# A two-layer RWKV block with an FP4 feed-forward on one core: three branches' second products in one burst, sums by channel block, pair products two levels at a time

## The chip, the cores and the metric

The kernel runs on one core of a Trainium2 chip. The metric is the device time of one execution in microseconds (us), the median of several runs. Engines are named as in the profile: PE is TensorE (PEld its weight loads), DVE is VectorE, ACT is ScalarE, POOL is GpSimd, SP is SyncE, which issues the DMAs.

## The reference

The input x is 2 x 4096 x 256, all in float32. It is normalised and modulated (`adaLN`), passed through two RWKV layers (a time mix and a channel mix each), added back with a gate, normalised again, and passed through a gated feed-forward whose inputs and weights are quantised to FP4 in blocks of 16 and dequantised. Cut to what matters here, a time mix is:

```python
sx = shift(x) - x
mix = tanh((x + sx * x_maa) @ tm_w1)              # 5 branches of E = 32 columns
mw, mk, mv, mr, mg = mix_f @ tm_w2[f]             # 32 -> 256, once for each branch f
wx = x + sx * (w_maa + mw)                        # and kx, vx, rx, gx likewise
r, k, v, g = sigmoid(rx @ Wr), kx @ Wk, vx @ Wv, silu(gx @ Wg)
w = exp(-exp(time_decay + tanh(wx @ td_w1) @ td_w2))
# for each head of 64 channels, step by step over t:
out_t = r_t @ (state + u * k_t^T v_t);  state = state * w_t + k_t^T v_t
h = h + (groupnorm(out) * g) @ Wo
```

The products `mix_f @ tm_w2[f]` are the "second products" of the title. The recurrence over t is what the pair products replace.

## The kernel before

**Tiles.** The work is cut into blocks of 256 time steps (`TT`), 16 for each of the two batches; each block passes both layers, so there are 64 time mixes and 64 channel mixes, and 32 feed-forwards in 64 chunks. A working tile ("slot", 128 partitions x 514 float32) holds one block in channel-major or time-major form; there are 36 slots, 4 double ones (`stock2`), 5 longer ones (`long`) and some tiny ones. PSUM has five banks that are handed out (`bank`), two banks for the pair products (`pa`) and one for `kv`.

**The planner.** Nothing is issued where it is written. Streams (one for each batch and layer, one for the feed-forward's inputs, one for each of its two chunks, one for its weights) record operations through `pl.tensor`, `pl.vector` and so on; `Plan.run` then gives them out one at a time by an estimate of when each could start (`weight`, `LAT`, `SAME`, `TURN`). Consecutive recordings on `pl.tensor` make one operation, a burst, which is given out whole and needs all its banks at once. The order of each engine's queue is therefore fixed when the kernel is built. Eight plans with different random ranks (`PLANS`, `JITTER`) are tried, and the one with the lowest estimated end is used. Because every operation is issued by `record` and `give_out`, the profile shows one line number (L294) for all of them, and the tiles' names tell them apart.

**Second products** (`time_mix`, L1006 to L1031). After the tanh, `mix_s` holds branches w, k, v, r in four groups of 32 partitions (`mixa`) and four copies of branch g (`mixb`). Three bursts follow: g's two products (one for each half of the output channels, in row groups 0 and 1, in two banks), `branch_pair(0, 3, ...)` for w and r (four products in row groups 0 and 3, two banks), and later `branch_pair(1, 2, ...)` for k and v. Each branch then goes through `to_input`: two SCALAR_TENSOR_TENSORs on DVE that read the bank, and one 128x512 sum on POOL that adds x.

**Pair products** (`wkv`, L837 to L965). A block of 128 steps is split into halves level by level (seven levels, h = 1, 2, ... 64). At each level PE multiplies r and k of paired halves into `pa`, and then DVE multiplies the r of each second half and the k of each first half by accumulated decays in place (`upd`). The products of a level have to read r and k before that level's update changes them, and after the update of the level before. The lines that set the bursts are these:

```python
        for l in range(7):
            h = 1 << l
            for m in {0: (), 1: (0, 1)}.get(l, (l,)):
                products(m)
```

Levels 0 and 1 share a burst, because level 0 reads copies of r and k with the bonus (`r0`, `k0`, two slots); levels 2 to 6 have one burst each. Levels 1 to 4 have 64 matmul records to a burst, level 5 has 32, level 6 has 16. Masks are applied by DVE (COPY_PREDICATED into `diag`) after levels 3 and 6. Only one block at a time is in this part (`head_lock`); its r and k lie in a double slot from `Wr`'s projection to the end of `wkv`.

**Channel mix and feed-forward** (L1125 to L1160, L1306 to L1394) are projections on PE with activations and FP4 steps (`fp4`, five DVE passes and one on ACT). `fp4` uses one `long` tile as scratch, and a chunk's hidden values and their transposes lie in two more.

## Time and profile before

| | |
|---|---|
| median of 3 runs | 3125.28 us (3124.25 to 3128.61) |
| the profiled execution | 3123.61 us |
| its span, first to last instruction | 3121.7 us |
| granted TensorE clock, mean | 0.981 |
| PE busy (matmul records) | 2984.9 us, 96%, 38460 records |
| PEld busy | 2412.9 us, 77% |
| DVE busy | 2365.4 us, 76%, 6146 instructions |
| ACT busy | 1615.4 us, 52%, 3362 instructions |
| POOL busy | 940.6 us, 30%, 888 instructions |

Busy times are unions over one profiled execution, from the first to the last instruction; 1.9 us of that execution lie outside the span. A float32 product shows as two matmul records. Matmuls are pipelined and their ends are modelled, so the time that a run of them takes is read from the start of its first to the start of whatever follows it. The span's first 60 us are mostly loads and the conditioning; the last 60 us are the last feed-forward chunks.

### The profile page before, as it was taken

Reading aid. Unit: us, or ns where it says so; the run is one execution under the profiler, and the core shown is the slowest. Engines: PE = TensorE matmul, PEld = TensorE weight load, DVE = VectorE, ACT = ScalarE, POOL = GpSimd, SP = SyncE. Lnnn points to the kernel's source line nnn. Section 1 sums busy time; section 2 is a strip of 40 time slices with the busy share of each in tenths; the row PEclk is TensorE's granted clock in tenths of the full one; section 3 lists DMA queues with packets and bytes.
Section 4 is the critical chain, followed back from the end, with each engine's and each line's share of the span. In section 5 each row is a group of like instructions: output and inputs, shape, how many; then the busy total and the mean of one; then the engine's idle time right before and its main releaser. Section 6 shows DMA issues by size and latency. Waiting matters only on the chain. (4 is left out here: it accounts for less than half of the span.)

```text
span 3121.7 us, 89338 instructions
## 1 busy us (share of the span) xinstructions
PE 2984.9 (96%) x38460; PEld 2412.9 (77%) x38460; DVE 2365.4 (76%) x6146; ACT 1615.4 (52%) x3362; POOL 940.6 (30%) x888
## 2 busy tenths in 40 slices
PE   6899999999999999999999999999999999999997
PEld 4777778778787777877778787787878778787775
DVE  6785778777877777778777787777777778766877
ACT  3565555545555556455454655546445455455442
POOL 2233323223233332332323233232332323331220
PEclk9899999999999999999999999999999999999989
DMA  4000000000000000000000000000000000000000
GB/s 141 20 14 5 10 7 15 7 15 7 9 12 7 16 8 11 11 6 17 5 11 11 5 18 5 14 8 9 13 6 17 5 8 15 9 9 9 8 13 11
DMA packets 35725, 42.53 MB, mean 14 GB/s; under 512 B 2817, under 2 KB 33537, under 8 KB 35329
## 3 DMA queue, kind: packets, MB, share of 16 engines
q1 hardware_dynamic: 35328, 36.81, 3.7%
q8 instruction: 302, 4.95, 0.7%
q14 instruction: 95, 0.77, 0.1%
HBM read 28.41 MB, written 8.39 MB: 12 GB/s over the span
## 5 line engine op out<-in xcount | busy, mean ns | idle before, releaser
L294 POOL TENSOR_TENSOR slot<-slot,slot 128x512 f32<-128x512 f32 (+1 forms) x448 | 508.9, 1152 | 961.5 <-DVE slot L294 682.0
L294 ACT ACTIVATE slot<-bank 128x512 f32<-128x512 f32 (+2 forms) x644 | 331.6, 519 | 682.8 <-PE bank L294 661.1
L294 POOL TENSOR_TENSOR tiny<-tiny,nhalf 128x2 f32<-128x2 f32 (+1 forms) x288 | 289.3, 1009 | 869.6 <-DVE tiny L294 789.4
L294 DVE TENSOR_TENSOR slot<-slot,slot 128x512 f32<-128x512 f32 x512 | 372.1, 728 | 110.2 <-PE pa L294 79.6
L294 PE MATMUL bank<-slot,small 32*128 32x256 f32 (+3 forms) x2816 | 393.3, 361 | 8.9 <-DVE slot L294 4.4
L294 PE MATMUL bank<-slot,cWk 128*128 128x256 f32 x1536 | 367.9, 385 | 2.5 <-DVE slot L294 2.0
L294 PE MATMUL bank<-cWv,slot 128*128 128x256 f32 x1536 | 343.8, 380 | 0.0
L294 PEld LDWEIGHTS pa<-slot 64*32 64x32 f32 x19456 | 224.0, 109 | 154.2 <-DVE diag L294 54.2
L294 PEld LDWEIGHTS bank<-slot,small 32*128 32x128 f32 (+3 forms) x2816 | 272.3, 178 | 88.3 <-issue 33.8
L294 PEld LDWEIGHTS bank<-slot,cWk 128*128 128x128 f32 x1536 | 284.5, 191 | 46.9 <-DVE slot L294 4.3
L294 PEld LDWEIGHTS bank<-cWv,slot 128*128 128x128 f32 x1536 | 289.2, 190 | 39.8 <-issue 0.3
L294 PE MATMUL pa<-slot 64*32 64x16 f32 x19456 | 266.2, 191 | 43.0 <-DVE diag L294 23.7
L294 ACT ACTIVATE slot<-bank,small 128x256 f32<-128x256 f32 (+1 forms) x640 | 248.4, 449 | 111.6 <-PE bank L294 109.9
L294 DVE SCALAR_TENSOR_TENSOR slot<-bank,small,slot 128x256 f32<-128x256 f32 x640 | 271.8, 473 | 24.9 <-PE bank L294 23.9
L294 DVE TENSOR_TENSOR slot<-slot,bank 128x512 f32<-128x512 f32 x192 | 131.0, 682 | 189.3 <-PE bank L294 143.0
L294 POOL TENSOR_TENSOR slot<-slot 128x512 f32<-128x512 f32 x128 | 141.9, 1111 | 346.8 <-ACT slot L294 272.3
L294 ACT ACTIVATE slot<-slot 128x512 f32<-128x512 f32 x288 | 181.3, 633 | 42.8 <-DVE slot L294 38.0
L294 DVE TENSOR_TENSOR long<-long,bank 128x352 f32<-128x352 f32 x256 | 131.1, 514 | 93.0 <-ACT long L294 69.8
L294 DVE SCALAR_TENSOR_TENSOR slot<-slot,small,slot 128x256 f32<-128x256 f32 x384 | 186.7, 518 | 16.8 <-POOL slot L294 16.7
L294 PE MATMUL bank<-ident,slot 128*128 128x128 f32 x1152 | 178.0, 283 | 14.0 <-ACT slot L294 8.6
L294 ACT COPY slot<-bank 128x512 f32<-128x512 f32 x224 | 130.3, 586 | 111.3 <-PE bank L294 107.3
L294 PE MATMUL bank<-wd,long 128*128 128x256 f32 x768 | 184.7, 391 | 1.2 <-ACT long L294 1.2
(106 smaller groups left out, 5362.5 us busy)
## 6 DMA issues: line engine op xcount, KB each, us to landing
slot<-in_L_attn_x_dram SPq DMA_DIRECT2D x64, 256.0 KB, 2.7
out_dram<-slot SPq DMA_DIRECT2D x64, 128.0 KB, 1.7
slot<-in_L_wmod_dram SPq DMA_DIRECT2D x6, 256.0 KB, 7.7
cWk<-in_L_attn_cWk_dram SPq DMA_DIRECT2D x2, 768.0 KB, 8.2
cWv<-in_L_attn_cWv_dram SPq DMA_DIRECT2D x2, 768.0 KB, 9.4
small<-in_small_dram SPq DMA_DIRECT2D x2, 718.0 KB, 8.3
long<-in_L_ffn_w_down_dram SPq DMA_DIRECT2D x2, 352.0 KB, 2.8
long<-in_L_ffn_w_gate_dram SPq DMA_DIRECT2D x5, 128.0 KB, 7.2
```

What stands on the lines that cost most here:

```text
L294: fn(*[real(v) for v in a], **{n: real(v) for n, v in k.items()})
```

## The change

- The second products of g, w and r are recorded as one burst of six products in row groups 1, 0 and 3 and in three banks, one bank for each branch; g now uses row group 1 for both halves of the channels. k and v stay a burst of their own. `to_input`'s sum on POOL is made for each half of the channels (two instructions of 128x256 in place of one of 128x512).
- In `wkv`, the products of levels 2 and 3 are one burst, and those of levels 4 and 5 another. For that the r and k from before an update must outlive it: the updates of level 2 and of level 4 write into another tile (`rk2`, kept for all blocks, in which level 0's copies lie too), and ACT copies the halves that the update does not touch. The other updates stay in place.
- Slots are reused in place where a result could overwrite an input (`x_s = xn_s`, `g_s = xg_s`, `hT_s = hb_s` and others), the counts of tiles go from 36, 4 and 5 to 37, 3 and 4, and streams that find no double or long tile wait.
- The planner's estimates of latencies change, and one plan is made in place of eight.

The diff, cut:

```diff
-SLOTS = 36
+SLOTS = 37
-PLANS, JITTER = 8, 8.0
-SLOTS2 = 4
+PLANS, JITTER = 1, 8.0
+SLOTS2 = 3
-LONG = 5
+LONG = 4
...
-    LAT = {"tensor": 170.0, "vector": 0.0, "scalar": 0.0, "gpsimd": 0.0, "sync": 2600.0, "load": 0.0}
+    LAT = {"tensor": 170.0, "vector": 120.0, "scalar": 60.0, "gpsimd": 200.0, "sync": 2600.0, "load": 0.0}
...
-    SAME = {"vector": 34.0, "scalar": 25.0, "gpsimd": 80.0}
+    SAME = {"vector": 84.0, "scalar": 25.0, "gpsimd": 80.0}
...
+        w["w2"] = [w2a[E * f : E * (f + 1), :] for f in range(4)] + [w2b[E : 2 * E, :]]
...
+    rk2 = keep.tile([P, 2 * J * TT], F32, name="rk2")
...
+    def pair_view(rk, h, n, changed=True):
+        v = rk[:, h : h + 1] if changed else rk[:, :1]
+        return bass.AP(
+            v.tensor, v.offset, [v.ap[0], [J * TT - h if changed else J * TT + h, 2], [2 * h, n], [1, h]]
+        )
...
-        r0_s, k0_s = take_slot(), take_slot()
-        r0, k0 = v4(r0_s), v4(k0_s)
+        r0, k0 = parts(rk2)
+        r, k = parts(rk)
...
+        place = {0: rk2, 1: rk, 2: rk, 3: rk2, 4: rk2, 5: rk, 6: rk, 7: rk}
         def products(l):
-            R, K = (r0, k0) if l == 0 else (r, k)
+            R, K = parts(place[l])
...
-            for m in {0: (), 1: (0, 1)}.get(l, (l,)):
+            for m in {1: (0, 1), 3: (2, 3), 5: (4, 5), 6: (6,)}.get(l, ()):
                 products(m)
...
-            upd = pair_view(rk, h, n)
+            here, there = place[l] if l else rk, place[l + 1]
+            if here is not there:
+                pl.scalar.copy(pair_view(there, h, n, False), pair_view(here, h, n, False))
             pl.vector.tensor_tensor(
-                upd, upd, tv...to_broadcast([P, 2, n, h]), ALU.mult
+                pair_view(there, h, n), pair_view(here, h, n), tv...to_broadcast([P, 2, n, h]), ALU.mult
             )
...
-            pl.gpsimd.tensor_tensor(m, m, x, ALU.add)
+            for j in range(J):
+                pl.gpsimd.tensor_tensor(m[:, j, :], m[:, j, :], x[:, j, :], ALU.add)
...
+        def branches(es, places):
+            bks, os = zip(*(pl.bank() for _ in es))
             for j in range(J):
-                for e, o in zip((f, g), os):
+                for e, o in zip(es, os):
+                    rows_, mix = (slice(E * e, E * (e + 1)), mixa) if e < 4 else (slice(E, 2 * E), mixb)
                     mm(
-                        o[:, j * TT : (j + 1) * TT], w["w2"][e][:, j * P : (j + 1) * P],
-                        mixa[E * e : E * (e + 1), :], True, True,
+                        o[:, j * TT : (j + 1) * TT], w["w2"][e][:, j * P : (j + 1) * P], mix[rows_, :],
+                        True, True,
                     )
...
-        bks, os = zip(*(pl.bank() for _ in range(2)))
-        for j in range(J):
-            js = slice(j * E, (j + 1) * E)
-            mm(os[j][:, :TT], w["w2b"][js, j * P : (j + 1) * P], mixb[js, :], True, True)
-        xg_s = to_input([o[:, :TT] for o in os], w["g_maa"])
...
-        xw_s, xr_s = branch_pair(0, 3, w["w_maa"], w["r_maa"])
+        xg_s, xw_s, xr_s = branches((4, 0, 3), (None, None, None))
+        yield
...
-        xk_s, xv_s = branch_pair(1, 2, w["k_maa"], w["v_maa"])
-        give(mix_s, x_s, sx_s)
+        xk_s, xv_s = branches((1, 2), (None, sx_s))
+        give(mix_s, x_s)
+        while not stock2:
+            yield
...
-        hT_s = pl.take(long)
+        hT_s = hb_s
```

More of the change, by code (lines that the diff above doesn't have):

```diff
@@ L600, in rwkv_adaln_fp4_kernel @@
         at += J * ED
-        w2a, w["w2b"], w["td2"] = (small[:, at + m * D : at + (m + 1) * D] for m in range(3))
-        w["w2"] = [w2a[E * f : E * (f + 1), :] for f in range(4)]
+        w2a, w2b, w["td2"] = (small[:, at + m * D : at + (m + 1) * D] for m in range(3))
+        w["w2"] = [w2a[E * f : E * (f + 1), :] for f in range(4)] + [w2b[E : 2 * E, :]]
         for n in ("Wr", "Wk", "Wv", "Wg", "Wo"):
@@ L763, in shifted @@
         bk, pt = to_channels(xn)
-        x_s = take_slot()
+        x_s = xn_s
         xT = x_s.rearrange("p (j t) -> p j t", j=J)
@@ L769, in shifted @@
         pl.close(bk)
-        give(xn_s)
         pl.vector.tensor_copy(car, xT[:, :, TT : TT + 1])
@@ L776, in shifted, with lerp @@
         return xT[:, :, 1:], sx, x_s, sx_s
-    def lerp(x, sx, maa):
-        m_s = take_slot()
+    def lerp(x, sx, maa, m_s=None):
+        m_s = m_s or take_slot()
         m = v3(m_s)
@@ L803, in proj_tok, with parts @@
         return bk, o
-    def pair_view(rk, h, n):
-        v = rk[:, h : h + 1]
-        return bass.AP(v.tensor, v.offset, [v.ap[0], [J * TT - h, 2], [2 * h, n], [1, h]])
+    def parts(rk):
+        return (
+            rk[:, m * J * TT : (m + 1) * J * TT].rearrange("p (c j t) -> p c j t", c=C, j=J) for m in range(2)
+        )
[3 more added lines that the diff above has]
+            v.tensor, v.offset, [v.ap[0], [J * TT - h if changed else J * TT + h, 2], [2 * h, n], [1, h]]
+        )
     def with_bonus(dst, src, odd, u):
@@ L840, in wkv @@
         rk = rk_s[:, : 2 * J * TT]
-        r, k = (rk[:, m * J * TT : (m + 1) * J * TT].rearrange(
-            "p (c j t) -> p c j t", c=C, j=J) for m in range(2))
         dec, v = v4(dec_s), v3(v_s)
@@ L878, in wkv @@
             h = 1 << l
-            for m in {0: (), 1: (0, 1)}.get(l, (l,)):
+            for m in {1: (0, 1), 3: (2, 3), 5: (4, 5), 6: (6,)}.get(l, ()):
                 products(m)
-            if l == 1:
-                give(r0_s, k0_s)
             n = C * J * P // (2 * h)
             tv = tot.rearrange("p (n two) -> p n two", two=2)
-            upd = pair_view(rk, h, n)
+            here, there = place[l] if l else rk, place[l + 1]
+            if here is not there:
+                pl.scalar.copy(pair_view(there, h, n, False), pair_view(here, h, n, False))
             pl.vector.tensor_tensor(
-                upd, upd, tv.rearrange("p n m -> p m n").unsqueeze(3).to_broadcast([P, 2, n, h]), ALU.mult
+                pair_view(there, h, n), pair_view(here, h, n), tv.rearrange("p n m -> p m n").unsqueeze(3).to_broadcast([P, 2, n, h]), ALU.mult
             )
@@ L915, in wkv @@
         give(dec_s)
+        r, k = parts(rk)
         tot = tot.rearrange("p (c j) -> p c j", c=C)
@@ L987, in time_mix @@
             mm(pm[:, TT : 2 * TT], w["w1"][:, k, P:], xx[:, k, :], k == 0, k == J - 1)
-        give(xx_s)
-        mix_s = take_slot()
+        mix_s = xx_s
         mixa, mixb = mix_s[:, :TT], mix_s[:, TT : 2 * TT]
@@ L993, in time_mix, with to_input @@
         yield
-        def to_input(o, maa):
-            m_s = take_slot()
+        def to_input(o, maa, m_s=None):
+            m_s = m_s or take_slot()
             m = v3(m_s)
@@ L1002, in to_input @@
                 )
-            pl.gpsimd.tensor_tensor(m, m, x, ALU.add)
-            return m_s
-        def branch_pair(f, g, maa_f, maa_g):
-            bks, os = zip(*(pl.bank() for _ in range(2)))
+            for j in range(J):
+                pl.gpsimd.tensor_tensor(m[:, j, :], m[:, j, :], x[:, j, :], ALU.add)
+            return m_s
+        def branches(es, places):
+            bks, os = zip(*(pl.bank() for _ in es))
             for j in range(J):
-                for e, o in zip((f, g), os):
-                    mm(
-                        o[:, j * TT : (j + 1) * TT], w["w2"][e][:, j * P : (j + 1) * P],
-                        mixa[E * e : E * (e + 1), :], True, True,
+                for e, o in zip(es, os):
+                    rows_, mix = (slice(E * e, E * (e + 1)), mixa) if e < 4 else (slice(E, 2 * E), mixb)
+                    mm(
+                        o[:, j * TT : (j + 1) * TT], w["w2"][e][:, j * P : (j + 1) * P], mix[rows_, :],
+                        True, True,
                     )
             ms = []
-            for bk, o, maa in zip(bks, os, (maa_f, maa_g)):
-                ms.append(to_input([o[:, j * TT : (j + 1) * TT] for j in range(J)], maa))
+            for e, bk, o, s in zip(es, bks, os, places):
+                ms.append(to_input([o[:, j * TT : (j + 1) * TT] for j in range(J)], w["wkvrg"[e] + "_maa"], s))
                 pl.close(bk)
             return ms
-        bks, os = zip(*(pl.bank() for _ in range(2)))
-        for j in range(J):
-            js = slice(j * E, (j + 1) * E)
-            mm(os[j][:, :TT], w["w2b"][js, j * P : (j + 1) * P], mixb[js, :], True, True)
-        xg_s = to_input([o[:, :TT] for o in os], w["g_maa"])
-        for bk in bks:
-            pl.close(bk)
+        xg_s, xw_s, xr_s = branches((4, 0, 3), (None, None, None))
         yield
-        xw_s, xr_s = branch_pair(0, 3, w["w_maa"], w["r_maa"])
         bk, pg = proj(w["Wg"], v3(xg_s))
-        give(xg_s)
-        g_s = take_slot()
+        g_s = xg_s
         g_t = v3(g_s)
@@ L1046, in time_mix @@
                 )
-        give(xw_s)
-        td_s = take_slot()
+        td_s = xw_s
         td = td_s[:, :P]
@@ L1096, in time_mix @@
             )
-        v_s = take_slot()
+        v_s = xv_s
         xv = v3(xv_s)
@@ L1101, in time_mix @@
         pl.close(bk)
-        give(xv_s)
         yield
@@ L1106, in time_mix @@
         bk, pt = to_channels(v3(o_s))
-        give(o_s)
-        oT_s = take_slot()
+        oT_s = o_s
         oT = v3(oT_s)
@@ L1128, in channel_mix @@
         xk, xk_s = lerp(x, sx, w["ck_maa"])
-        xr, xr_s = lerp(x, sx, w["cr_maa"])
-        give(x_s, sx_s)
+        xr, xr_s = lerp(x, sx, w["cr_maa"], sx_s)
+        give(x_s)
         yield
@@ L1139, in channel_mix @@
                     mm(o[:, m, :], w["cWk"][:, k, n0 : n0 + P], xk[:, k, :], k == 0, k == J - 1)
-            kks.append(take_slot())
+            kks.append(take_slot() if g < FD // P // 2 - 1 else xk_s)
             kg = v3(kks[-1])
@@ L1145, in channel_mix @@
             yield
-        give(xk_s)
-        sr_s = take_slot()
+        sr_s = xr_s
         sr = v3(sr_s)
@@ L1151, in channel_mix @@
         pl.close(bk)
-        give(xr_s)
         yield
@@ L1317, in ffn_inputs @@
             yield from layernorm_rows(x1, xn, rows["cb"][b], lambda c: rows["sb"][b])
+            while not long:
+                yield
             p_s = pl.take(long)
@@ L1320, in ffn_inputs @@
             long.append(p_s)
-            xq_s = take_slot()
+            xq_s = xn_s
             xqT = v3(xq_s)
@@ L1325, in ffn_inputs @@
             pl.close(bk)
-            give(xn_s)
             left = []
@@ L1345, in ffn_chunk @@
         x1, xqT = v3(x1_s), v3(xq_s)
+        while not long:
+            yield
         hb_s = pl.take(long)
@@ L1362, in ffn_chunk @@
             yield
+        while not long:
+            yield
         p_s = pl.take(long)
@@ L1377, in ffn_chunk @@
             yield
-        long.append(hb_s)
         bk, y = pl.bank()
```

## The prediction

> **What bounds the kernel now.** I read the page first, then the busy time by stage, then PE's timeline at places where the changed bursts stand alone, then the groups by shape. From the page:

> ```profile
> span 3121.7 us, 89338 instructions
> PE 2984.9 (96%) x38460; PEld 2412.9 (77%) x38460; DVE 2365.4 (76%) x6146; ACT 1615.4 (52%) x3362; POOL 940.6 (30%) x888
> PE   6899999999999999999999999999999999999997
> PEclk9899999999999999999999999999999999999989
> ```

> PE is at 9 in all but the first two slices and the last, and its clock is granted. The busy time by stage says how much of the rest can still be filled:

> ```profile
> 0.00:60.00 60.00, 33.87 (x298) 20.36 (x299) 34.31 (x111) 15.15 (x33) 12.95 (x34) 0.89 0.50 176
> 60.00:200.00 140.00, 124.00 (x1792) 100.91 (x1781) 112.53 (x326) 74.76 (x165) 45.15 (x41) 0.94 0.07 19
> 200.00:2900.00 2700.00, 2634.78 (x34827) 2138.58 (x34808) 2050.71 (x5330) 1438.80 (x2995) 838.81 (x772) 0.99 0.03 10
> 2900.00:3060.00 160.00, 148.32 (x1425) 120.32 (x1424) 125.88 (x298) 73.86 (x145) 37.63 (x36) 0.93 0.03 10
> 3060.00:3122.00 62.00, 43.98 (x176) 32.77 (x174) 41.96 (x83) 12.88 (x25) 6.05 (x8) 0.89 0.04 13
> ```

> The columns are length, then busy time of PE, PEld, DVE, ACT, POOL, then clock. Between 200 and 2900 us PE is without work for 65 us of 2700 (2.4%); the start costs 42 us and the last 222 us cost 30. So the time is PE's queue, and what counts is how long a burst keeps PE, start to start. PE's timeline (start, length, run) shows that:

> ```profile
> 424.13 0.70 PE L294 MATMUL bank<-slot,small 32*128 32x256 f32 x4
> 424.76 1.99 PE L294 MATMUL bank<-Wv,slot 128*128 128x256 f32 x8
> ...
> 427.12 1.13 PE L294 MATMUL bank<-slot,small 32*128 32x256 f32 x8
> 428.19 0.48 PE L294 MATMUL bank<-slot,Wg 128*128 128x256 f32 x1
> ```

> ```profile
> 546.71 1.89 PE L294 MATMUL bank<-slot,cWk 128*128 128x256 f32 x8
> 548.54 0.73 PE L294 MATMUL pa<-slot 64*32 64x16 f32 x64
> 549.20 1.45 PE L294 MATMUL bank<-wg,slot 128*128 128x352 f32 x4
> ```

> ```profile
> 1505.88 1.89 PE L294 MATMUL bank<-slot,small 128*128 128x256 f32 x8
> 1507.61 1.35 PE L294 MATMUL bank<-wg,slot 128*128 128x352 f32 x4
> ```

> g's burst alone (x4, two products side by side) takes 0.63 us; four products in two row groups (x8) take 1.06, that is one more round of 0.43. A level's pair products (x64) take 0.66. Eight full records take 1.73 ahead of full records and 1.83 ahead of a burst of another shape: entering a burst costs 0.10. The joint burst of levels 0 and 1 shows in the busy time of `pa` alone, 128 records from 586.82 to the next run at 588.03:

> ```profile
> 586.82:588.02 1.20, 1.20 (x128) 1.18 (x128) 0.00 (x0) 0.00 (x0) 1.00 0.05 14
> ```

> [...]

> **Second products.** Counted over the trace's records, the 64 time mixes make 18 runs of four records (g alone), 74 of eight, 40 of twelve and 7 longer, so g's burst stands alone 18 times and next to another one of its shape 46 times. In the new burst g's products run in a third row group beside w's and r's, and the burst should stay at 1.06. Saved: 18 x (0.63 + 0.10) + 46 x 0.43 = 33 us. That three groups run abreast is not shown by this shape. Bounds: if only two do, six products need three rounds, and what goes is the separate entry and tail, 18 x (0.73 - 0.43) = 5 us; if all do, 33. I take 33: the nearest row is `pa`'s, whose 64 records in 64x32 pieces (two row groups by four column groups) start every 8.6 ns (0.55 us for 64), far beyond two abreast.

> The burst needs three banks at once. That costs nothing as long as five are enough; the cover is that 46 of 64 times g's and the next burst already ran back to back with four banks between them, and PE's idle time before this shape is 3.7 us in all. Should the cover fail, every burst would wait for one bank's two DVE reads, 64 x 0.95 = 61 us, all of the gain.

> **Pair products.** A joint burst saves 0.66 + 0.66 - 1.21 = 0.11 us of tail, and one entry of 0.10. The trace holds 365 bursts on `pa` (some of the 384 already touch another); four for each of 64 blocks leave 256. 109 x 0.21 = 23 us. Waits go with the bursts: single-level ones lose 0.09 us each (0.08 ahead, 0.01 inside), joint ones of levels 0 and 1 also 0.09 (half ahead, half inside), so 109 x 0.09 = 10 us at most; since a joint burst waits for the later of two inputs I take 5. Bounds for both together: 7 (each new joint burst idles 0.12 inside, the mean of joint bursts over their median, 128 x 0.12 off 23) to 33; 28 taken.

> What these bursts wait for now is seen in the waits (total, times, longest):

> ```profile
> POOL slot L294 <- DVE slot L294: 691.8, 169, 22.9
> DVE slot L294 <- PE pa L294: 84.5, 92, 4.9
> PEld pa L294 <- DVE diag L294: 54.2, 81, 2.3
> ```

> DVE waits for the products before it may overwrite r and k (second line). With the second tile the updates of levels 2 and 4 wait for no burst, so two of six round trips between PE and DVE go from a block's chain. That shortens a chain that is not the bound: from the first pair product to the last `S` product a block takes 25.3 us (mean of 64), and a new one starts every 48.8 us (3122 / 64).

> **What is added** lies on other engines. From the groups by shape:

> ```profile
> L294 POOL TENSOR_TENSOR slot<-slot,slot 128x512 f32<-128x512 f32 x384 | 454.8, 1201 | 801.5 <-DVE slot L294 529.9 <-ACT slot L294 184.0 <-issue 36.0
> L294 POOL TENSOR_TENSOR slot<-slot,slot 128x256 f32<-128x256 f32 x64 | 54.6, 853 | 160.0 <-DVE slot L294 152.1 <-DVE tiny L294 3.4 <-PE bank L294 3.2
> L294 ACT ACTIVATE slot<-slot 128x512 f32<-128x512 f32 x288 | 181.3, 633 | 42.8 <-DVE slot L294 38.0
> ```

> ACT gets 128 copies of 128x512: 0.63 each by the last row, 81 us, 52% to 55%. The copy runs beside DVE's update (0.73), so it ends first unless ACT's queue is behind (a table load there takes 1.28 us; what a late copy costs is in the rival of the joint bursts); behind it on ACT wait evacuations of other blocks. POOL's 320 sums become 640: 320 x (2 x 0.853 - 1.201) = 162 us, 30% to 36%. A half starts one DVE instruction (0.47) sooner and the whole ends about level (0.47 against 0.51), so the projections behind see no difference; behind POOL's queue wait only other sums and the small pow instructions. DVE gets no instruction. No DMA is moved. Double tiles: from `Wr` to the end of `wkv` a block holds one for 52 us (27 + 25), which is 64 x 52 / 3122 = 1.1 of three in use, and at 57 of 64 starts at most two were; a fourth is not missed. `long`: a chunk now holds two at its peak and then one; with four instead of five tiles the input stream may wait in the last 60 us, 0 to 5 us, counted as 0. One plan and other latencies change every queue's order; from the trace this has no price of its own, and its bounds are PE's idle time, halved (33 us less) or doubled (65 more) in the middle stretch. I take 0, because 97.6% busy leaves little that order could win.

> [...]

> **Sum.** 33 + 28 = 61 us. The profiled execution took 3123.6 us (span 3121.7, 1.9 around it), so 3062.6; the median of the runs is 1.7 above that execution, so 3064.

> **Rivals.**
> - Two row groups abreast only: 28 us of the 33 stay. 3092. Against it: the 8.6 ns above. 0.08.
> - More than the sum: the pair products reach their upper bound, and better latencies in the planner halve the middle's 65 us of idle time: 3064 - 5 - 33 = 3026. For it: PE's waits for `diag`, which a plan that knows DVE's latency would place later. 0.12.
> [...]
> - Slower, the joint bursts: PE's queue is in order, so a burst given out before its second level's update is done stops PE for that update, 0.73 us. 128 x 0.73 = 93: 3157. It decides from 61 / 128 = 0.48 us of new idle time for each joint burst. For it: one plan, and 81 waits for `diag` show that the planner does place bursts too early; against it, 0.09 in the joint bursts of now. 0.09.
> - Nothing, as PE's busy time were no bound: 3125. Against it: full records start every 0.216 us with a weight load of 0.19 in each, so 88% is all that the loads could show in a full queue, and PE's timeline has no gaps between its runs. 0.04.

> **Numbers.** The forecast has 0.63. A difference below 0.2% (6 us) is what a measurement of this kernel can't tell from none. Faster: 0.63 + 0.12 + 0.08 = 0.83; same 0.04; slower 0.09 + 0.04 = 0.13. The range 3022 to 3108 takes in the three faster cases with a margin for the plan, and leaves out the other three.

> **What would show it.** Right: PE's records stay at 38460 and its busy time falls to about 2925; runs of twelve records in the shape 32*128 take 1.06 to 1.07; the page shows POOL with 1208 instructions and ACT with 3490; bursts on `pa` have 128 and 96 records at 1.21 and 0.94 (128 less 32 records of 8.6 ns); idle time in the middle stays near 65 us. [...] Wrong altogether: PE busy falls as said, and the span does not.

## The result and the profile after

| | before | changed |
|---|---|---|
| median | 3125.01 us (3124.25 to 3128.61, 4 runs) | 3092.68 us (3082.84 to 3097.78, 4 runs) |
| ratio | | 0.9888, 95% interval 0.9862 to 0.9913 |
| the profiled execution | 3123.61 us | 3082.84 us, the fastest of the four |

The change makes the kernel faster by 32 us. The forecast was 61. The page of the changed kernel:

```profile
span 3081.1 us, 89987 instructions
PE 2920.0 (95%) x38460; PEld 2388.7 (78%) x38460; DVE 2345.6 (76%) x6146; ACT 1667.6 (54%) x3478; POOL 1015.7 (33%) x1208
PE   6899999999999999999999999999999989999997
PEclk8899999999999999999999999999999999999999
```

PE has the same 38460 records and 65 us less busy time (2984.9 to 2920.0). The span fell by only 40.6 us, so PE's time without work rose, from 136.8 to 161.1 us. The busy time by stage (length, then PE, PEld, DVE, ACT, POOL) says where:

```profile
60.00:200.00 140.00, 121.62 (x1908) 100.23 (x1910) 102.20 (x289) 71.73 (x155) 45.83 (x54) 0.86 0.06 18
200.00:2900.00 2700.00, 2609.03 (x34890) 2148.96 (x34886) 2067.78 (x5433) 1511.73 (x3148) 917.88 (x1071) 0.99 0.03 10
```

In the middle stretch PE now idles 91 us where it idled 65. The bursts themselves look as they were forecast. PE's timeline at a burst of three branches, and the busy time of `pa` at a joint burst of levels 2 and 3:

```profile
1498.63 1.14 PE L294 MATMUL bank<-slot,small 32*128 32x256 f32 x12
1499.70 0.51 PE L294 MATMUL pa<-rk 64*32 64x32 f32 x36
```

```profile
1591.78:1592.95 1.17, 1.17 (x128) 1.17 (x128) 0.00 (x0) 0.00 (x0) 1.00 0.33 106
```

Twelve records in three row groups take 1.07 us, against 1.06 for eight in two; 128 pair-product records fill 1.17 us of their 1.19. And from the changed kernel's groups by shape, what was added on POOL, ACT and DVE:

```profile
L294 POOL TENSOR_TENSOR slot<-slot,slot 128x256 f32<-128x256 f32 x704 | 494.2, 730 | 645.8 <-DVE slot L294 615.2 <-DVE tiny L294 20.1 <-PE bank L294 9.4
L294 DVE SCALAR_TENSOR_TENSOR slot<-slot,small,slot 128x256 f32<-128x256 f32 x384 | 183.4, 516 | 14.9 <-POOL slot L294 14.8
L294 DVE TENSOR_TENSOR rk<-slot,slot 128x512 f32<-128x512 f32 x64 | 46.7, 730 | 18.7 <-ACT rk L294 18.6
L294 ACT COPY rk<-slot 128x512 f32<-128x512 f32 x64 | 39.6, 618 | 62.9 <-DVE slot L294 54.6 <-DVE rk L294 7.9
```

The half sums are cheaper than the row they were priced from (730 ns against 853), and the update of level 2, third line, waits for ACT's copy. The DVE instructions with two SBUF inputs, second line, did not get longer on average; before the change their row was this:

```profile
L294 DVE SCALAR_TENSOR_TENSOR slot<-slot,small,slot 128x256 f32<-128x256 f32 x384 | 186.7, 518 | 16.8 <-POOL slot L294 16.7
```

### The profile page after: what moved, and what is told of

Read it like the earlier page. It is cut to its first block, busy times and chain, and to the rows that moved or that the text cites. A ratio compares the mean times of both kernels' runs of the same rounds, so it can differ in the third digit from the quotient of the medians.

```text
span 3081.1 us, 89987 instructions
## 1 busy us (share of the span) xinstructions
PE 2920.0 (95%) x38460; PEld 2388.7 (78%) x38460; DVE 2345.6 (76%) x6146; ACT 1667.6 (54%) x3478; POOL 1015.7 (33%) x1208
## 5 line engine op out<-in xcount | busy, mean ns | idle before, releaser
L294 POOL TENSOR_TENSOR slot<-slot,slot 128x256 f32<-128x256 f32 (+1 forms) x768 | 578.1, 780 | 819.1 <-DVE slot L294 615.2
L294 ACT ACTIVATE slot<-bank 128x512 f32<-128x512 f32 (+2 forms) x644 | 334.3, 521 | 594.5 <-PE bank L294 563.4
L294 POOL TENSOR_TENSOR tiny<-tiny,nhalf 128x2 f32<-128x2 f32 (+1 forms) x288 | 296.9, 1034 | 874.6 <-DVE tiny L294 852.3
L294 PE MATMUL bank<-slot,cWk 128*128 128x256 f32 x1536 | 364.3, 385 | 4.5 <-DVE slot L294 4.5
L294 PE MATMUL bank<-slot,small 32*128 32x256 f32 (+3 forms) x2816 | 354.9, 359 | 10.3 <-DVE slot L294 6.9
L294 PE MATMUL bank<-cWv,slot 128*128 128x256 f32 x1536 | 342.4, 379 | 0.0
L294 PEld LDWEIGHTS bank<-slot,cWk 128*128 128x128 f32 x1536 | 288.1, 192 | 50.4 <-DVE slot L294 6.5
L294 ACT ACTIVATE slot<-bank,small 128x256 f32<-128x256 f32 (+1 forms) x640 | 250.9, 453 | 138.8 <-PE bank L294 128.7
L294 PEld LDWEIGHTS bank<-cWv,slot 128*128 128x128 f32 x1536 | 290.5, 190 | 39.7 <-issue 0.3
L294 PEld LDWEIGHTS bank<-slot,small 32*128 32x128 f32 (+3 forms) x2816 | 248.5, 178 | 86.2 <-issue 33.9
L294 DVE TENSOR_TENSOR slot<-slot,bank 128x512 f32<-128x512 f32 x192 | 130.7, 681 | 227.2 <-PE bank L294 193.5
L294 DVE TENSOR_TENSOR slot<-slot,slot 128x512 f32<-128x512 f32 x320 | 229.2, 718 | 82.2 <-PE pa L294 46.1
L294 DVE SCALAR_TENSOR_TENSOR slot<-bank,small,slot 128x256 f32<-128x256 f32 x640 | 265.1, 474 | 16.3 <-PE bank L294 16.0
L294 POOL TENSOR_TENSOR slot<-slot 128x512 f32<-128x512 f32 x128 | 140.3, 1098 | 358.4 <-ACT slot L294 253.5
L294 PEld LDWEIGHTS pa<-slot 64*32 64x32 f32 x11264 | 143.5, 109 | 79.9 <-DVE diag L294 35.2
L294 PE MATMUL pa<-slot 64*32 64x16 f32 x11264 | 171.6, 193 | 33.9 <-DVE diag L294 18.8
L294 PE MATMUL bank<-ident,slot 128*128 128x128 f32 x1152 | 176.1, 280 | 22.3 <-DVE slot L294 14.1
L294 DVE SCALAR_TENSOR_TENSOR slot<-slot,small,slot 128x256 f32<-128x256 f32 x384 | 183.4, 516 | 14.9 <-POOL slot L294 14.8
L294 ACT ACTIVATE slot<-slot 128x512 f32<-128x512 f32 x288 | 182.4, 636 | 21.9 <-DVE slot L294 17.3
L294 ACT ACTIVATE slot<-slot,tiny 128x256 f32<-128x256 f32 x256 | 141.6, 596 | 93.3 <-DVE tiny L294 89.9
L294 PE MATMUL bank<-wd,long 128*128 128x256 f32 x768 | 183.0, 389 | 2.2 <-ACT long L294 2.2
L294 PEld LDWEIGHTS bank<-ident,slot 128*128 128x128 f32 x1152 | 136.0, 143 | 57.8 <-DVE slot L294 19.6
```

Source lines behind the costliest of these rows:

```text
L294: fn(*[real(v) for v in a], **{n: real(v) for n, v in k.items()})
```

## The experiments

Three quantities tell the runs apart. The clock records of each trace give the spells in which the granted clock was one half. Full records (128x256) follow each other every 216 ns in the median at full clock and every 427 at one half, before and after alike, so half of the part of these spells in which PE was busy is the time that PE lost to the clock: 49 us before, 52 after. (The span times one minus the mean granted clock, 58 and 59 us, also counts spells in which PE had nothing to do.) PE's busy time less that loss is the work in its queue at full clock; the span less the busy time is idle time. Each experiment's ratio is against the kernel before, run beside it on the same chip (its medians there were 3130 to 3133 us), and the other columns are from its one profiled execution.

| run | ratio, 95% interval | span | PE busy | idle | clock loss | work |
|---|---|---|---|---|---|---|
| before | 1 | 3121.7 | 2984.9 | 137 | 49 | 2936 |
| changed | 0.9888 (0.9862 to 0.9913) | 3081.1 | 2920.0 | 161 | 52 | 2868 |
| e1 single bursts | 1.0321 (1.0306 to 1.0336) | 3233.6 | 2999.7 | 234 | 115 | 2885 |
| e2 g apart | 1.0040 (1.0028 to 1.0052) | 3146.1 | 2971.6 | 174 | 76 | 2896 |
| e3 whole sums | 1.0131 (1.0114 to 1.0148) | 3169.0 | 2958.1 | 211 | 88 | 2870 |
| e4 changed, best of 8 | 0.9870 (0.9857 to 0.9882) | 3086.9 | 2923.4 | 163 | 55 | 2868 |
| e5 changed, ranks 1 | 0.9975 (0.9962 to 0.9988) | 3124.4 | 2943.5 | 181 | 69 | 2874 |
| e6 changed, ranks 2 | 1.0076 (1.0049 to 1.0103) | 3147.4 | 2941.1 | 206 | 65 | 2876 |
| e7 before, ranks 1 | 1.0118 (1.0093 to 1.0144) | 3166.1 | 3002.0 | 164 | 57 | 2945 |
| e8 before, ranks 2 | 1.0223 (1.0190 to 1.0256) | 3198.7 | 3013.8 | 185 | 68 | 2945 |
| e9 single bursts, best of 8 | 1.0210 (1.0195 to 1.0225) | 3191.0 | 2978.0 | 213 | 88 | 2890 |
| e10 whole sums, best of 8 | 0.9990 (0.9979 to 1.0001) | 3129.9 | 2949.6 | 180 | 69 | 2881 |
| e11 old latencies, best of 8 | 0.9999 (0.9986 to 1.0012) | 3118.0 | 2932.5 | 185 | 57 | 2875 |
| e12 changed, ranks 41 | 0.9915 (0.9895 to 0.9935) | 3103.0 | 2941.2 | 162 | 66 | 2875 |

**e1, e2, e3, e4: one part undone each, and eight plans.** The first theory was that the work terms of the sum hold and the 26 us of new idle time in the middle come from the planner's edits.

```diff
e1 -            for m in {1: (0, 1), 3: (2, 3), 5: (4, 5), 6: (6,)}.get(l, ()):
e1 +            for m in {0: (), 1: (0, 1)}.get(l, (l,)):
e2 -        xg_s, xw_s, xr_s = branches((4, 0, 3), (None, None, None))
e2 +        w["w2b"] = w2b
...
e2 +        bks, os = zip(*(pl.bank() for _ in range(2)))
e2 +        for j in range(J):
e2 +            js = slice(j * E, (j + 1) * E)
e2 +            mm(os[j][:, :TT], w["w2b"][js, j * P : (j + 1) * P], mixb[js, :], True, True)
e2 +        xg_s = to_input([o[:, :TT] for o in os], w["g_maa"])
...
e2 +        xw_s, xr_s = branches((0, 3), (None, None))
e3 -            for j in range(J):
e3 -                pl.gpsimd.tensor_tensor(m[:, j, :], m[:, j, :], x[:, j, :], ALU.add)
e3 +            pl.gpsimd.tensor_tensor(m, m, x, ALU.add)
e4 -PLANS, JITTER = 1, 8.0
e4 +PLANS, JITTER = 8, 8.0
```

> The changed kernel with one burst for each of levels 2 to 5, its second tile, copies, planner and all else kept. Work theory (the burst terms of the sum are right, and the 26 us of new PE idle time between 200 and 2900 us come from the planner's edits): PE's busy time goes from 2920 to about 2943 us, idle time in the middle stays near 91 us, time 0.996 of the kernel before. Joint-burst theory (the new idle time is joint bursts that wait for the later of two inputs): busy time rises as much but idle time falls to about 65, time 0.988, as the change.

> The changed kernel with g's second products in a burst of their own, as before (two row groups, two banks). Work theory: runs of twelve records at 1.07 us go, runs of four at 0.63 come back, PE's busy time rises by 33 us to about 2953 us, idle time unchanged, time 0.999 of the kernel before. If three banks at once held PE up, idle time would fall from 91 us to about 65 and the time would be 0.991.

> The changed kernel with one 128x512 sum on POOL for each branch. Work theory: POOL's busy time falls by about 75 us, PE's stays at 2920, time 0.989 of the kernel before, as the change. [...] If the halves help (a projection starts earlier), the time is 0.993 or more.

> The changed kernel with the best of eight plans in place of one. If the new idle time is the one plan's bad luck: PE idle in the middle falls from 91 us to about 65, time 0.980 of the kernel before. If it belongs to the bursts, the sums or the latencies, whatever the plan: idle time 80 to 100 us, time 0.987 to 0.991. PE's busy time stays at 2920 in both.

The time of e1 missed every expectation, e3 went far past its last, and e2 came out half a percent above the work theory's 0.999. The work moves much as the work theory has it, by 16 us in e1 (23 were expected), 27 in e2 (33) and 1 in e3 (0). But each part undone cost more than its work: idle time rises by 73, 13 and 50 us, clock loss by 63, 25 and 37. e4 chose plan number 0 out of eight, which is the changed kernel's own (DVE, ACT and POOL run the same instructions in the same order in both traces), so it is a repeat of the change: 0.9870 beside 0.9888, with the same work. The edit from eight plans to one did nothing here. That left another reading: number 0 is a good plan for the changed kernel, as for the kernel before, whose eight plans also give number 0, and after any edit the same number is an ordinary one.

**e5 to e8: other plans of the same two kernels.** Nothing but the random ranks differs.

```diff
-    best = min(range(PLANS), key=lambda seed: plan(seed, True))
+    best = 1          # e5 and e7; 2 in e6 and e8
+    plan(best, True)
```

> The changed kernel, every recorded operation as it was, but planned with random ranks of number 1 in place of number 0: only the order in the queues differs. Order theory (a part undone cost more than its own work because its plan fell out worse, and plans differ by tens of us of PE idle time and half-clock time): same full-clock work on PE, idle time and clock loss 20 to 80 us more than with number 0, time 0.994 to 1.012 of the kernel before. Work theory (order is worth little, 97.6% busy): within 10 us of the change, 0.986 to 0.992.

> As the run before, with ranks of number 2. Order theory: 0.994 to 1.015, and not the same as number 1. Work theory: 0.986 to 0.992.

> The kernel before, planned with ranks of number 1 alone in place of the best of eight. Order theory: 20 to 80 us slower than the kernel before, 1.006 to 1.026, and slower than the changed kernel with the same ranks by some 55 us, the work that the change takes from PE. Work theory: within 10 us of the kernel before, 0.997 to 1.003.

> The kernel before with ranks of number 2. Order theory: 1.006 to 1.03, and slower than the changed kernel with the same ranks by some 55 us. Work theory: 0.997 to 1.003.

The order theory holds in all four. The same operations in another order cost 1.0% and 2.0% (0.9975 and 1.0076 over the mean of the two runs with number 0, 0.988), and 1.2% and 2.2% in the kernel before. The work column hardly sees the order: 2868 to 2876 in the changed kernel, 2936 to 2945 before. At equal ranks the change is worth 32 to 40 us with number 0, 43 with number 1 (3168.49 to 3125.83) and 47 with number 2 (3201.68 to 3154.82), a little less than the 55 expected. It is made the same way each time: 68, 71 and 70 us less work, and 24, 17 and 21 us more idle time. So the change's effect is not luck of the plan, and neither is the idle time that it adds.

**e9, e10, e11: parts undone, each with its best plan of eight.** e9 has the edit of e1 and e10 that of e3; e11 takes back the planner's latencies.

```diff
e9, e10, e11 +    best = 5          # e9; 3 in e10 and e11: the lowest estimate of ranks 0 to 7
e11 -    LAT = {"tensor": 170.0, "vector": 120.0, "scalar": 60.0, "gpsimd": 200.0, ...}
e11 +    LAT = {"tensor": 170.0, "vector": 0.0, "scalar": 0.0, "gpsimd": 0.0, ...}
e11 -    SAME = {"vector": 84.0, ...}
e11 +    SAME = {"vector": 34.0, ...}
```

> As e1 (one burst for each of levels 2 to 5, the rest of the change kept), but with the best of eight plans by the planner's estimate, as both kernels of the case had. Work theory with order taken out: PE busy 20 to 30 us over the change's 2920 (entries and tails come back), span minus PE busy as with the change (161 us), time 0.994 to 0.998 of the kernel before. Joint-burst theory (the joint bursts are what idles PE): span minus busy falls to about 140, time 0.988. If e1's loss was the bursts' and not its plan's: 1.02 or more.

> As e3 (one 128x512 sum on POOL for each branch, the rest of the change kept), with the best of eight plans. Order theory (e3's loss was its plan): 0.988 to 0.998 of the kernel before, PE busy about 2920 to 2935. If the halves themselves are worth time (a projection's first product need not wait for the whole sum), it stays at 1.005 or above, with PE idle time behind POOL.

> The changed kernel with the planner's latencies of the kernel before, best of eight plans. If the 21 us of idle time that the change adds at equal ranks come from the new latencies: span minus PE busy falls from 161 to about 140 us and the time is 0.980 to 0.984 of the kernel before. If the new latencies keep idle time down: span minus busy 180 us or more, 0.994 or above. If they are worth nothing: 0.985 to 0.991.

e9 is the case that its expectation put last. With the second tile but without joint bursts the kernel is 2.1% (e9) and 3.2% (e1) slower than before, outside everything that four plans of the changed kernel gave (0.987 to 1.008, with e12). PE's timeline in e9 (start, length, run, idle time ahead and who ended it) shows one reason:

```profile
1141.12 0.73 PE L294 MATMUL pa<-slot 64*32 64x16 f32 x64
1142.64 0.85 PE L294 MATMUL pa<-rk 64*32 64x16 f32 x64 [0.79 <-DVE tiny L294]
1143.42 0.48 PE L294 MATMUL bank<-slot,cWk 128*128 128x256 f32 x1
```

Level 2's burst is followed at once by level 3's, and PE stands for 0.79 us between them. The planner puts them side by side: 47 of e9's blocks have both levels without other work between, with 0.45 us of idle time inside on average, where the changed kernel has 0.03 inside its 64 joint bursts. Idle time ahead of and inside pair products is 86 us in e9 and 84 in e1, against 50 in the changed kernel and 47 before. So, in a kernel with the second tile and in both plans of it that were tried, the recording of two levels as one operation is worth much more than the entries and tails that the forecast counted. Idle time there explains 35 of e9's 52 us of new idle time; the clock loss (36 us) and 22 us of work come on top. Both tests keep the second tile and the copies; the pair products put back whole, in place, were not tried.

e10 comes out between its two expectations. It takes back a little over half of e3's loss (from 1.013 to 0.999, where the changed kernel gives 0.988), so at least that part was the plan's. Here PE waits 16.8 us for POOL at the output projection:

```profile
L294 PE MATMUL bank<-Wo,slot 128*128 128x256 f32 x512 | 127.5, 395 | 17.2 <-POOL slot L294 16.8 <-ACT long L294 0.2
```

In the changed kernel this row waits 9.8 us for POOL, and in e3, which has whole sums too, 5.0. So this wait goes with the plan and not with the size of the sums, and whether the halves are worth the 1.1% can't be told from these plans. For e2, with g apart, no other plan was run; how much of its loss beyond the 27 us of work is its plan's stays open. e11 gives 0.9999, with 7 us more work and 24 us more idle time than the change, as expected if the new latencies keep idle time down; but a difference of 1.2% again lies within what plans differ by. What it does show is that the old latencies, in the plan chosen by them, do not remove the added idle time.

**e12: a plan that the planner itself puts ahead.** Only the number of the ranks differs from the change.

> The changed kernel with ranks of number 41, which the planner's own estimate puts first of 56 (6 us ahead of number 0; numbers 1 and 2 stand 10 and 42 us behind number 0 by it, and were 35 and 62 us slower than it by ratio on the chip). If the estimate orders plans rightly over such small steps: the same or up to 20 us faster than the change, 0.980 to 0.988 of the kernel before, PE busy 2915 to 2925, span minus busy 140 to 160. If it only tells good plans from bad: 0.988 to 0.998.

0.9915: the second expectation, and not faster than the change (0.9870 and 0.9888). Idle time is the change's (162 us beside 161), but the profiled execution lost 14 us more to the clock. The estimate separates number 0 from numbers 1 and 2, but not plans within 6 us. No version faster than the changed kernel was found.

## Why the prediction was right or wrong

The direction, and the reason for it, held: PE is the bound, and the time fell because its queue got shorter. 3092.68 lies in the range; the gain was half of the forecast. In the profiled execution the work fell by 68 us where 56 were counted, but idle time rose by 24 us where it was to fall by 5, and the clock took 3 more; that leaves 41 us, of which the median of the runs shows 32. That the time equals the 3092 of the rival with two row groups abreast is chance, as that rival's mechanism fell. Point by point:

- *Second products, 33 us.* Right. Start to start and without idle time, all runs of this shape took 173.5 us before and 141.3 after: 32 us. Three row groups run abreast (1.07 us for six products against 1.06 for four, where a third round of 0.43 would have made it 1.49), so the rival of two abreast fell. With three banks at once PE waited 7.3 us ahead of this shape in place of 3.7, not 61. e2 agrees: with g apart the runs of this shape take 168.1 us, 27 more.
- *Pair products, 23 us of entries and tails.* The count held: 365 bursts became 254, and those of 128 and 96 records take 1.21 and 0.95 us (1.21 and 0.94 were said). The price was too low. Together the two terms are 56 us, and the work fell by 68, 71 and 70 us at the three ranks. At full clock the second products took 33, 35 and 32 of it and the runs on `pa` 15, 14 and 16, where tails were put at 12. The other 20 to 22 us lie in all other shapes, most of it in the full products of the channel mix and the feed-forward, where entries were put at 11. PE's queue changes shape 149 times less often (2553 to 2404), more than the 109 bursts and 18 runs of g that were counted, which fits; no run separates it.
- *Waits that go with the bursts, 5 us off.* This is the term that was mis-sized, sign included. Idle time at the pair products did not fall with the number of bursts (47.1 to 50.4 us), and PE's idle time as a whole rose by 24 us in place of falling by 5. At equal ranks it rose by 17 to 24. These are the waits that moved most, one line from before and three from the changed kernel:

```profile
PE bank L294 <- DVE slot L294: 25.9, 19, 13.3
```

```profile
DVE slot L294 <- PE pa L294: 46.1, 57, 2.5
PEld pa L294 <- DVE diag L294: 45.6, 57, 2.6
PE bank L294 <- DVE slot L294: 43.2, 33, 13.8
```

  DVE's waits for pair products fell from 84.5 to 46.1 us and the weight loads' waits for `diag` from 54.2 to 45.6, as the change would have it; what grew is PE's waits for other DVE results ahead of a bank (25.9 to 43.2), and by the engine waited for, PE's idle time rose for DVE (80 to 91), ACT (32 to 41) and POOL (11 to 15) alike. By what PE does next, three rows grew at each of the three ranks: the idle time ahead of the transposes `bank<-ident,slot` (by 8, 6 and 7 us), of the `kv` products (by 5 each time) and of the second products (by 4 to 6); ahead of the transposes `bank<-ident,long` it fell (by 8, 16 and 10). So much of the added idle time lies in the same places each time, and its cause stays open. It fits a PE with less work among neighbours that got no less, but that was only argued: single bursts, whole sums and old latencies each left idle time higher still, and fewer tiles (`SLOTS2`, `LONG`) and the copies were not tried.
- *The copy lies beside the update, at no cost.* Half right. At level 4 the update starts before the copy's end in 57 of 64 blocks; at level 2 it does so in 15 only, and in the median starts 33 ns after that end. That puts up to 0.62 us into a block's chain, 18.6 us of DVE's idle time, in a chain that still shortened from 25.3 to 21.6 us and is not the bound. PE's own waits for what ACT writes to that tile are 5.1 us. ACT has 3478 instructions and not the 3490 that were said, because its table loads fell from 127 to 115.
- *One plan and other latencies, 0, because 97.6% busy leaves little that order could win.* The zero was right for the plan count, which chose the same plan, but the reason was wrong: order can lose a great deal. The bounds given (33 less, 65 more) are about what plans differ by.
- *The sum against the median.* The 61 us assumed that the changed kernel's runs stand to its profile as before's did (1.7 us above). Its four runs spread over 15 us, and follow the granted clock: spans of 3081.1, 3085.9, 3096.0 and 3096.0 at 0.981, 0.978, 0.974 and 0.975. The profile showed 40.6 us, the median 32.
- *The slower rivals.* One of them, at 0.04, was that the added sums on POOL hold DVE up. No run shows that they cost time in this way: POOL's busy time rose by 75 us in place of 162, and the DVE row with two SBUF inputs did not get longer (518 ns to 516). Of its 384 instructions, the 75 before that have POOL work beside more than 0.3 of their time take 701 ns on average and the 297 that have none 473; after, it is 642 for 95 and 474 for 282. The 640 that read a bank take 473 and 474, with POOL work beside them or without. Joint bursts that wait inside: the wait that was feared there (0.48 us to decide) is 0.03 us inside the burst of levels 2 and 3; 0.32 us ahead of it is spent instead, 21 us in all. It is the single bursts of e1 and e9 that wait inside.
- *Nothing, as PE's busy time were no bound.* This rival fell: with 65 us less busy time the span fell by 40.6, and the weight loads' share hardly moved (77% to 78%).

## What to carry to other kernels

Where one engine's queue is the bound, split the span into its work at full clock, its idle time and its clock loss. Here the edits moved the first by an amount that could be counted in the main from burst lengths (56 us counted, 68 to 71 measured), and the order of the queue moved the other two by up to nearly as much again. When the order is made by a planner, compare a change at several plans of both kernels before crediting or blaming a part; plans of one kernel differ by 1% to 2% here, as much as the change itself or more. In this kernel two dependent bursts that the planner may put side by side are better recorded as one operation that starts when both are ready.
